# Row sums of softmax weights: a TensorE product with ones against folding by accumulating transfers

## Chip, cores and metric

The kernel runs on one core of a Trainium2 chip, in single precision. The metric is the device time of one execution in microseconds (us). Before the change it is 2455.27 us, the median of three runs (2454.65 to 2456.39).

## What is computed

Two graph layers with residual and layer norm follow one another. The change touches only the attention of the second: 16 batches, 1024 nodes, 256 channels in 4 heads.

```python
# x: 16 x 1024 x 256 after the first layer; adj: 1024 x 1024
g  = relu(einsum('bcn,bnm->bcm', transpose(x), adj * A_s(x)) * para)      # queries
k, v = split(x @ kv_w)                                                   # keys, values
attn = softmax(einsum('bhnd,bhmd->bhnm', q, k) * scale, axis=-1)
out  = einsum('bhnm,bhmd->bhnd', attn, v)
x = layernorm(x + out)
```

A softmax row is divided by the sum of its exponentials. The kernel doesn't divide the weights; it divides the output, so it needs, for each head and query, the sum over 1024 keys.

## The kernel before: the parts concerned

The schedule is one long list for 16 batches, software-pipelined: while batch b attends, the rows of batch b + 2 are normalised and the queries, keys and values of batch b + 1 made. A batch is 16 steps; a step does two of eight key blocks of 128 for one pair of heads and half the queries (512, a "half batch"). So four steps are one pair of heads (`NT // 2`), and eight are a half batch. Two steps are a slot, and the loop takes two slots (four steps) per turn: first the pieces put in these slots, then four steps of scores, exponentials, sums and products with the values.

In `scores` keys lie on the partitions and queries in the free dimension, so exponentials of one query are spread over partitions. VectorE adds the key blocks to one tile per pair, 128 partitions x (2 heads x 512 queries):

```python
accp = right("accp", 2)
...
def sums(g):
    b, hf, pair, cp = step(g)
    ...
    if cp == 0:
        ACC[b, hf, pair] = accp.tile([P, 2, FB], F32, tag="acc", name=f"acc{g}")
        nc.vector.tensor_add(ACC[b, hf, pair], E[g, 0], E[g, 1])
    else:
        for a in range(2):
            nc.vector.tensor_add(ACC[b, hf, pair], ACC[b, hf, pair], E[g, a])
```

What is left is a sum over 128 partitions. TensorE makes it with a matrix of ones, four products per half batch, each in its own 32 columns of the array; ScalarE copies the result, and four transfers put eight equal rows per head below the output in DRAM:

```python
def dens(b, hf):
    p = ps_t.tile([P, FB], F32, tag="t", name="pd")
    for pair in range(NP):
        acc = ACC.pop((b, hf, pair))
        for h in range(2):
            k = 32 * (2 * pair + h)
            more = EX.get((b, hf, pair), [])
            for n, t in enumerate(more + [acc]):
                nc.tensor.matmul(p[k : k + 32, :], ones32, t[:, h, :], start=n == 0, stop=n == len(more))
    DT[b, hf] = otp.tile([P, FB], F32, tag="dt", bufs=1, name=f"dt{b}_{hf}")
    nc.scalar.copy(DT[b, hf], p)
    if not by_pe(b, hf):                      # all but the last half batch
        for k in range(HEADS):
            put_o(b, hf, slice(C + k * DR, C + (k + 1) * DR), DT[b, hf][32 * k : 32 * k + DR, :])
```

Output and sums go through DRAM (`put_o`, `fetch_o`) because the way back, with VectorE's 32 x 32 transpose, turns them to one query per partition. `DR` is 8, so the sum of a head arrives as eight equal numbers, of which one is taken:

```python
def finish_a(b, j):
    ...
    nc.vector.transpose(t..., OB.pop((b, j))...)
    nc.vector.reciprocal(rd, t[:, :, C:].rearrange("p a (h r) -> p a h r", r=DR)[:, :, :, 0])
    p = r = t[:, :, :C]
    ...
    nc.vector.tensor_mul(r..., p..., rd...)          # divide
    nc.vector.tensor_add(r, r, x1s.pop((b, j)))      # residual
    mv, rs = ln_stats(sm, r, f"z{b}_{j}")            # moments on VectorE, square root on GpSimd
    ...                                              # two small GpSimd operations
```

GpSimd also scales the rows of batch b + 2 in place, between their load and VectorE's transpose of them:

```python
def bn2_q(b, j):
    y = yts[b, j].rearrange("p a (d n) -> p a d n", n=Q)
    for k, op in enumerate((OP.mult, OP.add)):
        ...
        nc.gpsimd.tensor_tensor(y, y, sc, op)
```

All transfers are issued from the sync engine, in order. The slots of the pieces of one half batch (`t = (hf + 1) * (NC // NH)`, that is 4 and 8 of the 8 slots of a batch):

```python
put(b, t, dens, b, hf)
...
if b * NH + hf < B * NH - 3:
    t_f, t_a, t_b = (t + 1, t + 2 + k, t + 6 + k) if hf == 0 else (t + 1, t + 4 + k, t + 6 + k)
...
put(b, t_f, fetch_o, b, j); put(b, t_a, finish_a, b, j); put(b, t_b, finish_b, b, j)
```

Of the kernel before, what the change touches and what calls it, by code (L numbers as in the profile page):

```python
# [11 lines left out]
OP = mybir.AluOpType  # L12
AX = mybir.AxisListType
# [3 lines left out]
P = 128  # L17
# [5 lines left out]
def gnn_norm_attention_kernel(  # L23
# [16 lines left out]
    nc = tc.nc  # L40
    B, N, C = x.shape
# [5 lines left out]
    NH = N // FB  # L47
# [38 lines left out]
    DR = 8  # L86
# [42 lines left out]
    with ExitStack() as l0:  # L129
# [33 lines left out]
        with ExitStack() as ph1:  # L163
# [9 lines left out]
            for i in range(0, NT, 2):  # L173
                t = hp.tile([P, 2, N], F32, tag="h", name=f"A{i}")
# [29 lines left out]
            for h in range(NH):  # L204
                rows = range(h * KB, (h + 1) * KB)
# [37 lines left out]
            for c in range(HT):  # L243
                p = ps.tile([P, FB], F32, tag="a", name="pw1")
# [3 lines left out]
            for c in range(CT):  # L248
                p = ps.tile([P, FB], F32, tag="a", name="pw2")
# [149 lines left out]
            for f in range(HT):  # L399
                for h in range(NH):  # L400
# [3 lines left out]
                    p = hidden(B - 1, h, f)  # L404
# [5 lines left out]
        right = lambda name, bufs: ctx.enter_context(tc.tile_pool(name=name, bufs=bufs, side="right"))  # L410
        keep = right("keep", 1)
        ldp = right("ldp", LDP)
        accp = right("accp", 2)
        RD = keep.tile([P, B * NT + 1, HEADS], F32, name="RD")
        ones32 = keep.tile([P, 32], F32, name="ones32")
        stq = keep.tile([P, 2, C // Q], F32, name="stq")
# [45 lines left out]
        with ExitStack() as ph2:  # L462
# [69 lines left out]
            for f in range(KF, HT):  # L532
                t = hT[u][:, f, :]
# [5 lines left out]
            for k, pair in enumerate(pairs):  # L539
# [4 lines left out]
                if not ahead:  # L544
                    for j in range(LDP):
                        load(0, j)
                    for j in range(LDP, NT // 2):
                        t = accp.tile([P, 2, FB], F32, tag="acc", name=f"first{j}")
# [14 lines left out]
    NP = HEADS // 2  # L563
# [17 lines left out]
    def fast():  # L581
      with ExitStack() as fx:
# [16 lines left out]
        kTs, qTs, vs, S, E, ACC, O, OT, DT = {}, {}, {}, {}, {}, {}, {}, {}, {}  # L599
# [228 lines left out]
        def by_pe(b, hf):  # L828
            return b == B - 1 and hf == NH - 1

        def attend(g):
            b, hf, pair, cp = step(g)
            if cp == 0:
                O[b, hf, pair] = [ps_t.tile([P, FB], F32, tag="t", name=f"o{g}_{r}") for r in range(2)]
            for a in range(2):
                cb = 2 * cp + a
                for r in range(2):
                    for h in range(2):
                        nc.tensor.matmul(  # L839
                            O[b, hf, pair][r][h * HD : (h + 1) * HD, :],  # L840
                            vs[b][r * HD : (r + 1) * HD, cb, pair * P + h * HD : pair * P + (h + 1) * HD],
                            E[g, a][r * HD : (r + 1) * HD, h, :],
                            start=(cb == 0),
                            stop=(cb == NT - 1),
                        )
                E.pop((g, a))
            if cp == NT // 2 - 1:
                t = otp.tile([P, FB], F32, tag=f"ot{pair}", bufs=1, name=f"ot{g}")
                o = O.pop((b, hf, pair))
                nc.scalar.copy(t, o[0])  # L850
                nc.vector.tensor_add(t, o[1], t)  # L851
                if by_pe(b, hf):
                    OT[b, hf, pair] = t
                else:
                    put_o(b, hf, slice(pair * P, (pair + 1) * P), t)

        def put_o(b, hf, rows_, t):
# [53 lines left out]
        def finish_a(b, j):  # L911
            hf, k = divmod(2 * j, KB)
            pool_r = (rp, "r") if b < B - 1 or not by_pe(b, hf) else (x1p, "x1")
            rd = RD[:, b * NT + 2 * j : b * NT + 2 * j + 2, :]
            if by_pe(b, hf):
                r = pool_r[0].tile([P, 2, C], F32, tag=pool_r[1], name=f"r_{b}_{j}")
                p = OB.pop((b, j))
            else:
                t = pool_r[0].tile([P, 2, CD], F32, tag=pool_r[1], name=f"r_{b}_{j}")
                nc.vector.transpose(  # L920
                    t.rearrange("p a c -> p (a c)"), OB.pop((b, j)).rearrange("p a c -> p (a c)")
                )
                nc.vector.reciprocal(rd, t[:, :, C:].rearrange("p a (h r) -> p a h r", r=DR)[:, :, :, 0])
                p = r = t[:, :, :C]
            if j == NT // 2 - 1 and by_pe(b, hf):

                for a in range(2):
                    for h in range(HEADS):
                        nc.scalar.mul(r[:, a, ts(h, HD)], p[:, a, ts(h, HD)], rd[:, a, h : h + 1])
            else:  # L930
                nc.vector.tensor_mul(
                    r.rearrange("p a (h d) -> p a h d", h=HEADS),
                    p.rearrange("p a (h d) -> p a h d", h=HEADS),
                    rd.unsqueeze(3).to_broadcast([P, 2, HEADS, HD]),
                )
# [47 lines left out]
        NC = NS // 2  # L983
        NK = NT // 2
        at, between = {}, {}

        def put(w, t, f, *a):
            at.setdefault(w * NC + t, []).append((f, a))
# [4 lines left out]
        for b in range(B):  # L993

            for hf in range(NH):
                t = (hf + 1) * (NC // NH)
                put(b, t, dens, b, hf)
                if by_pe(b, hf):
                    put(b, t, recips, b, hf)
                for k in range(KB // 2):  # L1000
                    j = hf * (KB // 2) + k

                    if b * NH + hf < B * NH - 3:
                        t_f, t_a, t_b = (t + 1, t + 2 + k, t + 6 + k) if hf == 0 else (t + 1, t + 4 + k, t + 6 + k)
                    elif not by_pe(b, hf):

                        t_f, t_a, t_b = t, t + 2 * k, t + 2 + 2 * k if b < B - 1 else (t + 2, NC + 1)[k]
                        if b == B - 1 and k == 0:
                            between[(b * NC + t_b) * 2 + NK // 2] = [(finish_b, (b, j))]
                            t_b = None  # L1010
                    else:
                        t_f, t_a, t_b = t, t + 1 + k, t + 2 + k
                    put(b, t_f, back if by_pe(b, hf) else fetch_o, b, j)
                    if t_a == t:
                        between[(b * NC + t) * 2 + NK // 2] = [(finish_a, (b, j))]
                    else:
                        put(b, t_a, finish_a, b, j)
                    if t_b is not None:
                        put(b, t_b, finish_b, b, j)
            if b == 0:  # L1020
                continue

            if b > 1:
                put(b - 2, 2, begin, b)
                for j in range(NT // 2):
                    put(b - 2, j, load, b, j)
                    put(b - 2, j + 1, bn2_q, b, j)
                    put(b - 2, j + 2, rows, b, j)
                    put(b - 2, j + 2, ln1_a, b, j)
                    put(b - 2, j + 3, ln1_b, b, j)  # L1030
                    put(b - 2, j + 3, put_x1, b, j)
                    put(b - 2, 5 + j // 2 * 2, get_x1, b, j)
                    put(b - 2, min(6 + j, NC), x1_v, b, j)
                put(b - 2, NC - 2, means, b)
                put(b - 2, NC - 1, crow, b)

            i = 0
            for t, n in enumerate(WG):
                for i in range(i, i + n):
                    put(b - 1, t, gate, b, i)  # L1040
                i += 1
            kv = [(keys, (b, c, h)) for h in range(NH) for c in range(CT)]
            kv += [(values, (b, j)) for j in range(0, NT, 2)]
            for t, n in enumerate(KV):
                for _ in range(n):
                    f, a = kv.pop(0)
                    put(b - 1, t, f, *a)
            m = 0
            for t, n in enumerate(QG):
                for m in range(m, m + n):  # L1050
                    put(b - 1, NC - len(QG) + t, graph, b, m)
                m += 1
# [3 lines left out]
        nsteps = B * NS  # L1056


        order = (dens, recips, x1_t, finish_a, fetch_o, finish_b, x1_v, rows, ln1_a, ln1_b, put_x1, get_x1, means, load, crow)
        rank = {f: k for k, f in enumerate(order)}  # L1060
        short = (dens, recips, x1_t, back)

# [141 lines left out]
        for t in range(-NC // 2, max(max(at) // 2, nsteps // NK - 1) + 1):  # L1204
# [3 lines left out]
            for k in range(len(now) + 1):  # L1208
                if k == behind and 0 <= g < nsteps:
                    sums(g)  # L1210
                if k < len(now):
                    f, a = now[k]
# [177 lines left out]
```

## Time and profile before

| | before |
|---|---|
| time, median of 3 | 2455.27 us |
| span of the profiled execution | 2454.0 us |
| busy: TensorE / VectorE / ScalarE / GpSimd | 2411.8 / 1811.3 / 1094.8 / 776.9 us |
| mean busy share of the 16 DMA engines (sync queue) | 43.0% |
| TensorE clock granted, mean | 0.995 of full |

The first 880 us are the first layer and the two batch norms; from about 880 us on the attention runs, until 2454 us. In the profile PE is TensorE's matmul, PEld its weight load, DVE VectorE, ACT ScalarE, POOL GpSimd, SPq the sync engine's queue. A group's line gives the line of the kernel, the engine, the operation and "output<-inputs"; a letter L and a number name a line of the kernel. A share of busy time is an average over stages that have different limits.

### The profile page before, as it was taken

Reading aid. Unit: us, or ns where it says so; the run is one execution under the profiler, and the core shown is the slowest. Engines: PE = TensorE matmul, PEld = TensorE weight load, DVE = VectorE, ACT = ScalarE, POOL = GpSimd, SP = SyncE. Lnnn points to the kernel's source line nnn. Section 1 sums busy time; section 2 is a strip of 40 time slices with the busy share of each in tenths; the row PEclk is TensorE's granted clock in tenths of the full one; section 3 lists DMA queues with packets and bytes.
Section 4 is the critical chain, followed back from the end, with each engine's and each line's share of the span. In section 5 each row is a group of like instructions: output and inputs, shape, how many; then the busy total and the mean of one; then the engine's idle time right before and its main releaser. Section 6 shows DMA issues by size and latency. Waiting matters only on the chain. (4 is left out here: it accounts for less than half of the span.)

```text
span 2454.0 us, 33894 instructions
## 1 busy us (share of the span) xinstructions
PE 2411.8 (98%) x12225; PEld 1008.5 (41%) x12225; DVE 1811.3 (74%) x2584; ACT 1094.8 (45%) x1555; POOL 776.9 (32%) x826
## 2 busy tenths in 40 slices
PE   8999999999999899999999999999999999999997
PEld 4444444444344443443434434344343443443432
DVE  5555545556776777888788888888888888888677
ACT  2000000001554455564655646656566565564645
POOL 2222222231556521414224133232332323414013
PEclk9999999999999899999999999999999999999999
DMA  3122122222578543544545545545354453544222
GB/s 137 69 86 103 69 86 103 85 87 86 199 272 278 133 121 83 143 119 112 143 106 129 143 95 146 122 120 144 81 150 114 123 149 89 145 112 118 72 44 56
DMA packets 583951, 292.73 MB, mean 119 GB/s; under 512 B 407528, under 2 KB 556512, under 8 KB 576608
## 3 DMA queue, kind: packets, MB, share of 16 engines
q1 hardware_dynamic: 583776, 290.49, 43.0%
q8 instruction: 98, 1.61, 0.3%
q14 instruction: 77, 0.63, 0.1%
HBM read 194.46 MB, written 95.94 MB: 118 GB/s over the span
## 5 line engine op out<-in xcount | busy, mean ns | idle before, releaser
L809 ACT ACTIVATE e<-s 128x1024 f32<-128x1024 f32 x512 | 496.0, 1020 | 327.5 <-PE s L797 265.4
L824 DVE TENSOR_TENSOR acc<-acc,e 128x1024 f32<-128x1024 f32 x382 | 509.3, 1333 | 112.1 <-ACT e L809 85.4
L797 PE MATMUL s<-qT,kT 64*64 64x512 f32 x4096 | 490.7, 594 | 4.4 <-ACT e L809 1.7
L839 PE MATMUL o<-e,v 64*64 64x512 f32 x4096 | 485.3, 589 | 0.0
L771 PE MATMUL pg<-wg,x 128*128 128x512 f32 x960 | 426.5, 597 | 0.0
L624 POOL TENSOR_TENSOR yt<-yt,stq 128x512 f32<-128x512 f32 x120 | 185.2, 1544 | 406.4 <-DMA yt<-yT 239.8
L771 PEld LDWEIGHTS pg<-wg,x 128*128 128x128 f32 x960 | 178.7, 190 | 238.6 <-issue 237.4
L839 PEld LDWEIGHTS o<-e,v 64*64 64x64 f32 x4096 | 156.6, 133 | 282.9 <-issue 275.2
L797 PEld LDWEIGHTS s<-qT,kT 64*64 64x64 f32 x4096 | 147.1, 133 | 298.5 <-issue 254.2
L107 ACT COPY u<-pa 128x512 f32<-128x512 f32 x15 | 8.8, 586 | 475.3 <-PE pa L313 475.3
L66 POOL TENSOR_SCALAR rs_z<-mv_z 128x2 f32<-128x2 f32 x64 | 18.5, 290 | 470.5 <-DVE mv_z L573 470.4
L730 DVE SCALAR_TENSOR_TENSOR wg<-wg,adj 128x1024 f32<-128x1024 f32 x128 | 163.4, 1308 | 2.8
L313 PE MATMUL pa<-AhT,x 128*128 128x512 f32 x360 | 161.8, 592 | 0.0
L656 ACT ACTIVATE x<-x,nm_a,rs_a 128x256 f32<-128x256 f32 x128 | 75.8, 594 | 171.9 <-POOL nm_a L646 171.4
L851 DVE TENSOR_TENSOR ot<-o,ot 128x512 f32<-128x512 f32 x64 | 44.2, 691 | 127.5 <-ACT ot L850 127.5
L757 PE MATMUL pv<-kvw,x1T 128*128 128x256 f32 x512 | 118.7, 385 | 0.0
L746 PE MATMUL pk<-x1T,kvw 128*128 128x512 f32 x256 | 117.9, 604 | 0.0
L66 POOL TENSOR_SCALAR rs_a<-mv_a 128x2 f32<-128x2 f32 x64 | 38.0, 594 | 236.5 <-DVE mv_a L573 235.2
L344 PE MATMUL ph<-agg,SW 128*128 128x512 f32 x240 | 112.8, 592 | 0.0
L757 PEld LDWEIGHTS pv<-kvw,x1T 128*128 128x128 f32 x512 | 97.1, 192 | 31.8 <-issue 16.2
L313 PE MATMUL pa<-T,sx 128*128 128x512 f32 x240 | 107.9, 592 | 0.0
L313 PEld LDWEIGHTS pa<-AhT,x 128*128 128x128 f32 x360 | 68.4, 190 | 86.1 <-issue 86.1
(198 smaller groups left out, 3147.1 us busy)
## 6 DMA issues: line engine op xcount, KB each, us to landing
adj<-in_adj_dram SPq DMA_DIRECT2D x128, 512.0 KB
h<-hT SPq DMA_DIRECT2D x28, 1024.0 KB
hL<-h SPq DMA_DIRECT2D x28, 1024.0 KB
ob<-o SPq DMA_DIRECT2D x248, 72.0 KB
x<-in_x_dram SPq DMA_DIRECT2D x16, 1024.0 KB
yT<-y SPq DMA_DIRECT2D x64, 256.0 KB
out_dram<-r SPq DMA_DIRECT2D x64, 256.0 KB
xr<-in_x_dram SPq DMA_DIRECT2D x62, 256.0 KB
```

Source lines behind the costliest of these rows:

```text
L313: nc.tensor.matmul(p, xs[n][:, k, :], bs[n][:, k, :], start=(k == 0), stop=(k == KN - 1))
L344: nc.tensor.matmul(p, ws[n][:, ts(f, P)], bs[n], start=True, stop=True)
L624: nc.gpsimd.tensor_tensor(y, y, sc, op)
L656: nc.scalar.activation(r, r, AF.Identity, bias=nm[:, a : a + 1], scale=rs[:, a : a + 1], accum_out=css[b][:, i : i + 1])
L730: nc.vector.scalar_tensor_tensor(t, t, 1.0, adjs[b * NT + i], op0=OP.add, op1=OP.mult)
L746: nc.tensor.matmul(p, kvw[:, k, ts(c, P)], x1Ts[b][:, k, ts(h, FB)], start=(k == 0), stop=(k == CT - 1))
L757: nc.tensor.matmul(p[:, ts(a, C)], x1Ts[b][:, k, ts(j + a, P)], kvw[:, k, C:], start=(k == 0), stop=(k == CT - 1),)
L771: nc.tensor.matmul(pg[b], x1s[b, k // 2][:, k % 2, ts(c, P)], wgs[b, k][:, ts(h, FB)], start=(k == 0), stop=(k == NT - 1))
L797: nc.tensor.matmul(t[r * HD : (r + 1) * HD, h, :], kTs[b, pair][h * HD : (h + 1) * HD, ts(2 * cb + r, HD)], qTs[b, pair, hf][h * HD : (h + ...
L809: nc.scalar.activation(E[g, a], S.pop((g, a)), AF.Exp)
L824: nc.vector.tensor_add(ACC[b, hf, pair], ACC[b, hf, pair], E[g, a])
L839: nc.tensor.matmul(O[b, hf, pair][r][h * HD : (h + 1) * HD, :], vs[b][r * HD : (r + 1) * HD, cb, pair * P + h * HD : pair * P + (h + 1) * HD],
```

## The change

For all half batches but the last three there is no product with ones. Instead the upper half of the tile's partitions is added to the lower half by a transfer that accumulates, issued from GpSimd: 64 partitions on 64, then 32 on 32, 16 on 16 and 8 on 8. Eight partial sums per query and head are left. They are stored where the eight equal rows stood, and `finish_a` adds the eight numbers (one more VectorE reduction) before the reciprocal. A third `accp` buffer is there because a tile stays in use until its sums are stored. The first fold is a piece of the turn after the pair's last sum; the other three stand between that turn's steps; the store follows in the next turn. So the fetch comes two slots later, and for half 0 the first finishing step is moved between steps.

The purpose is to take the products off TensorE.

```diff
-        accp = right("accp", 2)
+        accp = right("accp", 3)
...
+        def by_dma(b, hf):
+            return b * NH + hf < B * NH - 3
+
+        def fold(b, hf, pair, n):
+            acc = ACC[b, hf, pair]
+            nc.gpsimd.dma_start(acc[:n], acc[n : 2 * n], accum_op=OP.add)
+
+        def put_den(b, hf, pair):
+            acc = ACC.pop((b, hf, pair))
+            for h in range(2):
+                r = C + (2 * pair + h) * DR
+                put_o(b, hf, slice(r, r + DR), acc[:DR, h, :])
...
-                nc.vector.reciprocal(rd, t[:, :, C:].rearrange("p a (h r) -> p a h r", r=DR)[:, :, :, 0])
+                den = t[:, :, C:].rearrange("p a (h r) -> p a h r", r=DR)
+                if by_dma(b, hf):
+                    nc.vector.tensor_reduce(rd, den, AX.X, OP.add)
+                    nc.vector.reciprocal(rd, rd)
+                else:
+                    nc.vector.reciprocal(rd, den[:, :, :, 0])
...
-                put(b, t, dens, b, hf)
+                if by_dma(b, hf):
+                    for pair in range(NP):
+
+                        s = b * NC + t + 2 * (pair - NP + 1)
+                        put(0, s + 1, fold, b, hf, pair, P // 2)
+                        for k in range(3):
+                            between.setdefault(2 * s + k, []).append((fold, (b, hf, pair, P // 4 >> k)))
+                        put(0, s + 2, put_den, b, hf, pair)
+                else:
+                    put(b, t, dens, b, hf)
...
                     if b * NH + hf < B * NH - 3:
-                        t_f, t_a, t_b = (t + 1, t + 2 + k, t + 6 + k) if hf == 0 else (t + 1, t + 4 + k, t + 6 + k)
+                        t_f, t_a, t_b = (t + 3, None, t + 6 + k) if hf == 0 else (t + 3, t + 4 + k, t + 6 + k)
+                        if hf == 0:
+                            between.setdefault((b * NC + t + 2) * 2 + 2 * k + 1, []).append((finish_a, (b, j)))
...
-        order = (dens, recips, x1_t, finish_a, fetch_o, ...
+        order = (dens, recips, x1_t, put_den, finish_a, fetch_o, ...
```

More of the change, by code (lines that the diff above doesn't have):

```diff
@@ L1008, in fast @@
                         if b == B - 1 and k == 0:
-                            between[(b * NC + t_b) * 2 + NK // 2] = [(finish_b, (b, j))]
+                            between.setdefault((b * NC + t_b) * 2 + NK // 2, []).append((finish_b, (b, j)))
                             t_b = None
@@ L1014, in fast @@
                     if t_a == t:
-                        between[(b * NC + t) * 2 + NK // 2] = [(finish_a, (b, j))]
-                    else:
+                        between.setdefault((b * NC + t) * 2 + NK // 2, []).append((finish_a, (b, j)))
+                    elif t_a is not None:
                         put(b, t_a, finish_a, b, j)
@@ L1056, in fast @@
         nsteps = B * NS
-        order = (dens, recips, x1_t, finish_a, fetch_o, finish_b, x1_v, rows, ln1_a, ln1_b, put_x1, get_x1, means, load, crow)
+        order = (dens, recips, x1_t, put_den, finish_a, fetch_o, finish_b, x1_v, rows, ln1_a, ln1_b, put_x1, get_x1, means, load, crow)
         rank = {f: k for k, f in enumerate(order)}
```

## The prediction

> **What bounds the kernel now.** I read the page's first part, busy time by engine:
>
> ```profile
> PE 2411.8 (98%) x12225; PEld 1008.5 (41%) x12225; DVE 1811.3 (74%) x2584; ACT 1094.8 (45%) x1555; POOL 776.9 (32%) x826
> ```
>
> TensorE is busy 98% of the span. That is an average over stages, so next I asked for the busy time of each engine in the attention stage alone, 900 to 2300 us, in the order PE, PEld, DVE, ACT, POOL, then granted clock, DMA share and GB/s:
>
> ```profile
> 900.00:2300.00 1400.00, 1398.16 (x8933) 557.40 (x8935) 1163.11 (x1590) 815.41 (x1134) 435.23 (x548) 1.00 0.50 123
> ```
>
> 1398.16 of 1400 us: TensorE never stops there, and the list of waits for TensorE between 900 and 2380 us is empty. VectorE has 237 us (17%) to spare, GpSimd 965 us (69%), the DMA engines half. So in this stage time is the sum of TensorE's work, and whatever is taken from TensorE comes off the end, as long as the others still keep ahead of it.
>
> Third, what the row-sum products cost. Instructions of the tile `pd` (min/median/max ns):
>
> ```profile
> L870 PE MATMUL pd<-acc,ones x256: 592/593/618, 924.0 to 2439.5; 128*32 128x512 f32 x128
> ```
>
> Of these 256 records each lasts 593 ns, but they must not be summed. The timeline of TensorE shows one stage of them (start, duration, group):
>
> ```profile
> 1272.92 1.98 PE L746 MATMUL pk<-x1T,kvw 128*128 128x512 f32 x4
> 1274.84 1.06 PE L870 MATMUL pd<-acc,ones 128*32 128x512 f32 x8
> 1275.84 5.42 PE L746 MATMUL pk<-x1T,kvw 128*128 128x512 f32 x12
> 1281.09 1.89 PE L757 MATMUL pv<-kvw,x1T 128*128 128x256 f32 x8
> ```
>
> One half batch has eight such records (four products, two records each), and they take 1274.84 to 1275.84, 1.00 us, together. There is a little more: the twelve `pk` records after them come at (1281.09 − 1275.84)/12 = 0.44 us each, so the four before should take 1.75 us, but the first `pd` starts 1.92 us after the first `pk`. A `pd` stage so costs 1.00 us plus about 0.17 us of changing over. The next one of the same kind is at 1375.37: a batch lasts 100.5 us, a half batch 50.3 us, one pair of heads (the unit in which sums are made and folded) 25.1 us.
>
> Last, GpSimd, because the new work goes through its queue (groups in that window: busy, mean ns, idle before and its releasers):
>
> ```profile
> L624 POOL TENSOR_TENSOR yt<-yt,stq 128x512 f32<-128x512 f32 x108 | 169.4, 1569 | 383.4 <-DMA yt<-yT 221.6 <-DMA o<-dt 110.0 <-DVE wg L730 47.7
> L66 POOL TENSOR_SCALAR rs_a<-mv_a 128x2 f32<-128x2 f32 x56 | 35.6, 635 | 221.7 <-DVE mv_a L573 220.5
> L66 POOL TENSOR_SCALAR rs_z<-mv_z 128x2 f32<-128x2 f32 x54 | 12.0, 223 | 321.4 <-DVE mv_z L573 321.4
> ```
>
> GpSimd has 435.23/1400 × 25.1 = 7.8 us of work per pair and otherwise waits for a load or for VectorE's moments. Its idle time is plentiful but lies between steps of a chain (scale the rows loaded, normalise) that VectorE waits for.
>
> **What the Trainium skill says.** TensorEngine Tiling (Array Packing), Key Properties: different tiles run in parallel, and changing the tiling mode drains TensorE. The trace agrees: eight 593 ns records in 1.00 us, and 0.17 us lost ahead of them. DMA: Bandwidth & Descriptors, Anatomy of one DMA — SWDGE (gpsimd) path: a DMA issued from GpSimd takes about 2.0 us plus bytes/436 GB/s, most of it waiting for the write to be confirmed. The kernel before issues none from GpSimd, so no run here shows it yet. Same page, Two DMAs through the same engine are not ordered: a DMA that reads what an earlier one wrote needs the issuing engine to wait for the earlier one's semaphore, so the waits between folds fall on GpSimd itself. SBUF — State Buffer, SBUF: two separate sides: GpSimd can't write descriptors while VectorE runs a 2-port operation. Of VectorE's costly groups here only the sign operation (L729, 69 × 846 ns in the window, 4%) and the scaling of queries can be of that kind; the 1.3 us sums have two inputs. I add nothing for it.
>
> **The change part by part.**
> Removed from TensorE: 32 − 3 = 29 half batches × (1.00 + 0.17) us = 34 us, 29 us without the changeover. It lies on the bound.
> Removed from ScalarE: 29 copies of `pd` at 0.589 us, 17 us. ScalarE is 58% busy in the stage: worth nothing directly.
> Added to VectorE: 58 reductions of 8 × 8 numbers. A reciprocal on 8 numbers takes 204 ns and statistics over 256 take 411 ns, so I estimate 0.25 us each, 15 us in all, in 237 us of room: nothing at the end.
> Added to GpSimd's queue: 29 × 2 pairs × 4 folds = 232 transfers, of 256, 128, 64 and 32 KB. By the skill's formula, estimates: 2.6 + 2.3 + 2.15 + 2.1 = 9.1 us per pair; GpSimd itself stands still for the first three, 7 us, and for four issues. That formula is for a copy on free DMA engines; an accumulating transfer reads the destination too, and the engines here are half busy, so I allow up to twice, 18 us. With the 7.8 us of old work that is 17 to 26 us out of 25.1 us. The lower half fits, the upper end doesn't.
> DMA engines: 58 × 480 KB = 28 MB more through engines that move 123 GB/s, about 20 GB/s over the stage. They have the room.
> Moved: the sums go to DRAM once per pair, after the last fold; the fetch of the output for half 0 comes two slots (half a half batch) later, and its first finishing step one and a half steps into the same loop turn. `accp` grows to three, since a sum stays until it is stored.
> Sum: 2455 − 34 = 2421 to 2455 − 29 = 2426 if nothing new is waited for. I choose 2427: the changeover kept in, some 5 us lost to short stalls.
>
> **The rivals.**
> (1) GpSimd becomes late, and VectorE with it. In each pair the first fold stands behind GpSimd's pieces, and the next turn's row scaling stands behind the last fold. In the trace, one turn has GpSimd's last piece end near 1322.9 us and the transpose of the rows that the next scaling feeds start at 1337.5 us: 14.6 us, of which the scaling takes 3.1. A chain up to some 11.5 us is free, a 15 us one delays VectorE by 3 to 4 us, once or twice per batch. VectorE has 17 us idle per batch and TensorE runs some three steps ahead in `e` buffers (six), so this much is absorbed. With an 18 us chain each turn begins with the backlog of the one before, GpSimd is the bound, and 26 − 25 us times 58 pairs plus stalls makes 2480 to 2560 us. For it: the room is nearly used up at the upper end. Against: the chain has to be twice the skill's figure.
> (2) The sync queue is held up. It is in order; the store of the sums waits for the last fold, and loads of rows, adjacency tiles and the output's fetch stand behind it. In the timeline this queue already idles until the attention output is ready (592.7 us in total), so a store that is ready a few us after that costs little. For half 0, though, the fetch and the step that needs it are now in one turn of 25 us: fold, store, read back, about 10 us. I expect VectorE to wait there some us per batch, within its 17 us. If not, 14 batches × 3 us = 42 us would take back the gain: about 2460.
> (3) TensorE's time isn't freed, because the products were hidden in gaps. The empty list of waits and 1398 of 1400 us busy speak against it; then 2455.
>
> **Range and chances.** Without trouble 2421 to 2426; light stalls up to 2440; rival 2 about 2460, rival 1 2480 and up. The gain can't reach 2% (49 us) since only 34 us are taken away, so faster by over 2% gets 0.03. Slower by over 2% (from 2504) needs rival 1 in full: 0.14. Range 2418 to 2488.
>
> **What would show it.** Right: `pd` has 24 + 8 records left; TensorE still above 99% in the stage; batch period 98.2 us instead of 100.5; GpSimd waiting for `acc` transfers without VectorE waiting for `yt`, `x1` or `ob`. Wrong: TensorE waiting for `e` or `qT`, VectorE waiting for DMA `ob` or for GpSimd `yt`, the sync queue waiting long for `acc`, GpSimd with hardly a gap; a fold of more than 5 us from issue to landing would do it.

## The result and the profile after

The changed kernel takes 2622.47 us (median of 4 runs, 2620.83 to 2625.65) against 2455.57 us for the kernel before on the same chip: a ratio of 1.0681, interval 1.0663 to 1.07. It is 167 us slower. The prediction said 2427 us and a range of 2418 to 2488: the measured time lies 134 us above the end of that range.

The products are gone as intended (TensorE has 11993 matmuls instead of 12225). What is left of TensorE's fullness, first on the page (busy time by engine) of the kernel after:

```profile
PE 2439.7 (93%) x11993; PEld 1017.8 (39%) x11993; DVE 1825.0 (70%) x2642; ACT 1081.5 (41%) x1526; POOL 983.3 (38%) x1058
```

and in the stage between 900 and 2300 us, columns as before (PE, PEld, DVE, ACT, POOL, granted clock, DMA share, GB/s):

```profile
900.00:2300.00 1400.00, 1282.12 (x7812) 510.08 (x7811) 1057.72 (x1480) 719.48 (x996) 570.43 (x702) 0.96 0.59 128
```

TensorE was busy for 1398.16 of these 1400 us; now it stands for 118 us of them, does 12.5% fewer matmuls in the same time (224 of the 1121 missing ones are the products themselves), and its granted clock has fallen from 1.00 to 0.96. Its list of waits between 900 and 2380 us was empty; in the kernel after, between 900 and 2500 us, it has two lines (total us, times, longest):

```profile
PE s L797 <- ACT e L809: 72.0, 14, 6.3
PE pk L746 <- DVE x1T L679: 57.8, 14, 4.1
```

One of each per batch. A batch, by the distance of the `pc` products that occur once in each, lasts 112.4 us (median) instead of 100.53. I call the first wait A, the second B.

**Wait A.** The timeline of the turn that handles the second pair of row blocks (start, duration, group, and in brackets the idle time before it and its releaser):

```profile
1812.53 0.94 POOL L839 DMA_DIRECT2D acc<-acc  x1
...
1823.61 0.18 DVE L573 BATCH_NORM_AGGREGATE mv_a<-st_a 128x2 f32<-128x6 f32 x1
...
1823.89 0.81 POOL L839 DMA_DIRECT2D acc<-acc  x1 [2.95 <-DMA acc<-acc]
...
1824.44 2.80 POOL L624 TENSOR_TENSOR yt<-yt,stq 128x512 f32<-128x512 f32 x2
...
1830.47 0.49 POOL L646 TENSOR_SCALAR nm_a<-mv_a,rs_a 128x1 f32<-128x1 f32 x2
...
1830.76 0.60 ACT L656 ACTIVATE x<-x,nm_a,rs_a 128x256 f32<-128x256 f32 x1 [14.12 <-POOL nm_a L646]
...
1831.94 1.91 ACT L809 ACTIVATE e<-s 128x1024 f32<-128x1024 f32 x2
...
1833.00 3.69 PE L797 MATMUL s<-qT,kT 64*64 64x512 f32 x16 [5.78 <-ACT e L809]
```

Read it from the bottom. TensorE waits 5.78 us for exponentials. ScalarE isn't short of time: it stood for 14.12 us at the normalisation of rows (L656), which comes ahead of the exponentials in its order and waits for `nm_a` (the shift that this normalisation adds, made by GpSimd from VectorE's moments `mv_a`). GpSimd makes `nm_a` late because the fold chain, 1812.53 to 1824.44, stands ahead of it in GpSimd's order, and after that the scaling of the next rows and GpSimd's part of a finishing step. The moments are ready at 1823.79, but GpSimd takes them up only at 1829.35, so 5.56 us of the wait are GpSimd's backlog. The rest is older than the change: in the kernel before, the longest wait of this kind is 7.8 us.

**Wait B.** The start of a batch, where the next keys are made:

```profile
1870.52 3.70 PE L746 MATMUL pk<-x1T,kvw 128*128 128x512 f32 x8
...
1871.84 0.77 DVE L936 STREAM_TRANSPOSE r<-ob 128x576 f32<-128x576 f32 x1
...
1875.15 0.40 DVE L572 BATCH_NORM_STATS2 st_z<-r 128x6 f32<-128x256 f32 x1
...
1876.90 1.30 DVE L679 STREAM_TRANSPOSE x1T<-xb 128x512 f32<-128x512 f32 x2
...
1878.34 5.37 PE L746 MATMUL pk<-x1T,kvw 128*128 128x512 f32 x8 [4.12 <-DVE x1T L679]
```

The second finishing step of half 0, which the change put between the last steps of a batch, occupies VectorE from 1871.84 to about 1875.8, and one addition to a row sum follows, so the transposes `x1T` for the keys start at 1876.90, some 5 us after VectorE reached this place.

**The clock.** The windows right before, at and after these waits:

```profile
1815.00:1826.00 11.00, 11.00 (x44) 4.47 (x47) 10.03 (x21) 1.64 (x5) 3.60 (x5) 1.00 0.33 54
...
1833.00:1837.00 4.00, 4.00 (x20) 1.29 (x24) 3.27 (x3) 2.06 (x3) 3.57 (x5) 0.50 0.77 148
1837.00:1841.00 4.00, 4.00 (x36) 1.27 (x32) 1.62 (x2) 1.63 (x2) 0.80 (x1) 0.85 0.70 113
...
1878.00:1884.00 6.00, 5.66 (x11) 2.62 (x12) 5.90 (x7) 1.89 (x3) 3.29 (x4) 0.72 0.84 201
```

After wait A TensorE runs for 4 us at half clock and 4 more at 0.85, after B 6 us at 0.72: 2.0 + 0.6 + 1.7 = 4.3 us lost. The Trainium skill, TensorE: Matmul & The Clock Gate, What's actually happening, says that the clock halves after at least one idle window of about 3.4 us and recovers after at least one busy window of that length. Here the trace agrees: half clock after a wait of 5.78 us, and for about 5 us from the moment work resumed (4 us, and 30% of the next 4). Shorter waits can do the same; the last section has them.

**The sum of a batch.** Per batch, wait A costs 72.0/14 = 5.1 us, B 57.8/14 = 4.1, the clock 4.3; the missing products give back 1.95 (measured below). 5.1 + 4.1 + 4.3 − 1.95 = 11.6, of 11.9 seen. Over the whole: the last `pc` starts at 2416.1 us instead of 2264.1, 152 us later, and from there to the end it is 202.9 instead of 189.9 us, 13 more: 165 us, the difference of the two spans (2619.0 and 2454.0).

**The folds** themselves are near what was estimated. The page's list of transfers (count, size, median us from issue to landing):

```profile
acc<-acc POOLq DMA_DIRECT2D x58, 256.0 KB, 4.4
...
acc<-acc POOLq DMA_DIRECT2D x58, 128.0 KB, 3.2
...
acc<-acc POOLq DMA_DIRECT2D x58, 64.0 KB, 2.9
acc<-acc POOLq DMA_DIRECT2D x58, 32.0 KB, 2.9
```

4.4 + 3.2 + 2.9 + 2.9 = 13.4 us, inside the 9.1 to 18 that was allowed for. The 9.1 that the prediction works out from the skill's formula is too short by a third here, and the measurement decides.

### The profile page after: what moved, and what is told of

It reads as the page before. It is cut to its first block, busy times and chain, and to the rows that moved or that the text cites. A ratio compares the mean times of both kernels' runs of the same rounds, so it can differ in the third digit from the quotient of the medians.

```text
span 2619.0 us, 33966 instructions
## 1 busy us (share of the span) xinstructions
PE 2439.7 (93%) x11993; PEld 1017.8 (39%) x11993; DVE 1825.0 (70%) x2642; ACT 1081.5 (41%) x1526; POOL 983.3 (38%) x1058
## 5 line engine op out<-in xcount | busy, mean ns | idle before, releaser
L824 DVE TENSOR_TENSOR acc<-acc,e 128x1024 f32<-128x1024 f32 x382 | 483.4, 1265 | 157.0 <-ACT e L809 133.7
L797 PE MATMUL s<-qT,kT 64*64 64x512 f32 x4096 | 515.2, 620 | 79.2 <-ACT e L809 76.5
L855 PE MATMUL o<-e,v 64*64 64x512 f32 x4096 | 495.0, 600 | 0.0
L839 POOL DMA_DIRECT2D acc<-acc x232 | 192.4, 845 | 512.1 <-DMA acc<-acc 506.9
L624 POOL TENSOR_TENSOR yt<-yt,stq 128x512 f32<-128x512 f32 x120 | 174.6, 1456 | 128.2 <-DMA yt<-yT 108.0
L746 PE MATMUL pk<-x1T,kvw 128*128 128x512 f32 x256 | 141.1, 704 | 57.8 <-DVE x1T L679 57.8
L656 ACT ACTIVATE x<-x,nm_a,rs_a 128x256 f32<-128x256 f32 x128 | 75.6, 592 | 267.1 <-POOL nm_a L646 267.1
L66 POOL TENSOR_SCALAR rs_z<-mv_z 128x2 f32<-128x2 f32 x64 | 46.9, 733 | 278.7 <-DVE mv_z L573 249.8
L746 PEld LDWEIGHTS pk<-x1T,kvw 128*128 128x128 f32 x256 | 54.4, 222 | 142.9 <-issue 131.3
```

The lines of the kernel that those rows point to most:

```text
L746: nc.tensor.matmul(p, kvw[:, k, ts(c, P)], x1Ts[b][:, k, ts(h, FB)], start=(k == 0), stop=(k == CT - 1))
L797: nc.tensor.matmul(t[r * HD : (r + 1) * HD, h, :], kTs[b, pair][h * HD : (h + 1) * HD, ts(2 * cb + r, HD)], qTs[b, pair, hf][h * HD : (h + ...
L839: nc.gpsimd.dma_start(acc[:n], acc[n : 2 * n], accum_op=OP.add)
L855: nc.tensor.matmul(O[b, hf, pair][r][h * HD : (h + 1) * HD, :], vs[b][r * HD : (r + 1) * HD, cb, pair * P + h * HD : pair * P + (h + 1) * HD],
```

## Experiments

The theory was that A and B are separate faults of order: A from the chain ahead of the row pieces on GpSimd, B from the moved finishing step on VectorE. Rivals: that folds cost what they cost wherever they stand (contention), or that the two waits are one path. In the expectations A and B are the waits above; C is a second path, VectorE to GpSimd to ScalarE, in the turn of the half-0 products, with no slack in the kernel before; D and E are explained where they come up.

### Without the folds, and without the change's other half

`e4_nofold`: the kernel after, with the 232 folds left out (only eight of 128 partitions are summed).

```diff
-            nc.gpsimd.dma_start(acc[:n], acc[n : 2 * n], accum_op=OP.add)
+            pass
```

> Changed kernel without the 232 folds: eight raw partial sums of 128 are stored, the rest is left out, so the output is not the reference's. Theory: A goes as GpSimd is never held, B stays: about 2515 us, like the run that moves the normalisation. Rival (folds cost through DMA engines and the sync queue, and B is their effect too): both stalls go, about 2425 us.

2532.62 us, 1.0315 (1.0294 to 1.0335), 105.4 to 106.2 us per batch. TensorE's waits, 900 to 2300 us:

```profile
PE pk L746 <- DVE x1T L679: 52.3, 13, 4.0
PE s L797 <- ACT e L809: 12.7, 12, 1.1
```

B is there in full, 4.0 us each, without a single fold: it is the order on VectorE. A shrinks from 5.1 to 1.1 us each. So the folds make most of A, and leaving them out is worth 90 us of the 167. ScalarE's longest wait for `nm_a` falls from 14.7 to 9.3 us. The other 77 us belong to the rest of the change; the next run takes its slots alone.

`e5_before_moved`: the kernel before, with products, and only the slots of the change (both fetches two slots later, half 0's first finishing steps between steps).

```diff
-                        t_f, t_a, t_b = (t + 1, t + 2 + k, t + 6 + k) if hf == 0 else (t + 1, t + 4 + k, t + 6 + k)
+                        t_f, t_a, t_b = (t + 3, None, t + 6 + k) if hf == 0 else (t + 3, t + 4 + k, t + 6 + k)
+                        if hf == 0:
+                            between.setdefault((b * NC + t + 2) * 2 + 2 * k + 1, []).append((finish_a, (b, j)))
...
```

> Kernel before, with its products and no folds; only the slots of half 0 are those of the change (fetch two slots later, finishing steps between the steps of the turn before the x1T transposes). Theory (B is an order on VectorE): the stall of 4 us before the keys is there in all 14 batches and some 1.7 us of low clock after it: 2455 + 81, about 2535 us. Rival (B comes only because the folds make the output's fetch late): within 10 us of 2455.

2483.55 us, 1.0113 (1.0093 to 1.0133), 102.31 us per batch. The slots alone cost 28 us, about a third of what was expected: B is only 1.5 us per batch (20.1 us in 13 waits, at most 1.6) and the granted clock stays at 1.00. So the 4 us of B come from the moved step together with something else. I can only argue what: without the products the turn is shorter, and VectorE has one more operation in each finishing step, a reduction of 0.22 us.

### Taking A away, taking B away

`e1_ln1b`: the kernel after; the normalisation of row block 2 (and its store) one slot later, which is the next turn; block 3 already stood in that slot.

```diff
-                    put(b - 2, j + 3, ln1_b, b, j)
-                    put(b - 2, j + 3, put_x1, b, j)
+                    put(b - 2, j + 3 if j < 2 else 6, ln1_b, b, j)
+                    put(b - 2, j + 3 if j < 2 else 6, put_x1, b, j)
```

> Changed kernel; ScalarE's normalisation of the third row block (the one that waits up to 14 us for GpSimd, ahead of the exponentials of its turn) comes one slot later, behind these exponentials. Theory (two stalls per batch, each followed by about 4 us at half clock: A, ScalarE held by GpSimd's folds; B, the x1T transposes standing behind the finishing step that was moved): A goes, B stays; A is 72.0/14 = 5.1 us of stall plus some 2.6 us of low clock per batch, 7.7 x 14 = 108 us: about 2515 us. Rival (sync queue held by the stores of the sums, and fuller DMA engines): nothing but an order on ScalarE is changed, so within 15 us of 2622.

2630.17 us, 1.0712 (1.0691 to 1.0733): A is gone and nothing is gained; TensorE now waits for `x1T`, 114.4 us in 10 waits.

`e12_after_ln`: the same question more gently: only blocks 0 and 2 move, to between the steps of their own turn, behind its first exponentials.

```diff
-                    put(b - 2, j + 3, ln1_b, b, j)
-                    put(b - 2, j + 3, put_x1, b, j)
+                    if j % 2:
+                        put(b - 2, j + 3, ln1_b, b, j)
+                        put(b - 2, j + 3, put_x1, b, j)
+                    else:
+                        g = (b - 2) * NS + 5 + 2 * j
+                        between.setdefault(g, []).extend([(ln1_b, (b, j)), (put_x1, (b, j))])
```

> Changed kernel, only the normalisation of row blocks 0 and 2 on ScalarE moved between the steps of its own turn (not a whole turn later, as in the first run, which made the output's fetch late). Theory: stall A goes, B stays at about 4 us: 2622 - 108, about 2515 us, 2500 to 2540. Rival (with A gone, B grows as in the first run, since the fold chain then ends later within the turn): 2590 to 2630.

2618.13 us, 1.0664 (1.0643 to 1.0686). Again A is gone (0.7 us in all) and B has grown (waits of TensorE and VectorE, 900 to 2300 us):

```profile
PE pk L746 <- DVE x1T L679: 113.4, 11, 13.4
...
DVE r L936 <- DMA ob<-o: 84.9, 11, 10.1
```

What VectorE now waits for is the output read back. The timelines of both kernels say why. The kernel after, from the chain that made A to the finishing step (the first line is the chain of half 0's first pair, the second that of its second pair, then its stored sums and the fetch):

```profile
1812.53 0.94 POOL L839 DMA_DIRECT2D acc<-acc  x1
...
1835.84 0.91 POOL L839 DMA_DIRECT2D acc<-acc  x1
...
1849.98 0.82 SPq L874 DMA_DIRECT2D o<-acc  x2
...
1852.47 4.67 SPq L922 DMA_DIRECT2D ob<-o  x8
```

and the same in this experiment, with the finishing step in the last line:

```profile
1807.99 0.93 POOL L839 DMA_DIRECT2D acc<-acc  x1
...
1835.19 0.94 POOL L839 DMA_DIRECT2D acc<-acc  x1
...
1848.70 0.64 SPq L874 DMA_DIRECT2D o<-acc  x2
...
1851.00 5.75 SPq L922 DMA_DIRECT2D ob<-o  x8
...
1856.29 0.78 DVE L936 STREAM_TRANSPOSE r<-ob 128x576 f32<-128x576 f32 x1 [8.01 <-DMA ob<-o]
```

On GpSimd stand, in order, the first pair's chain, the row pieces of the turn with their waits for VectorE, and the second pair's chain; then store, fetch, finishing step, transposes, keys. From the first chain's start to the keys it takes 1878.34 − 1812.53 = 65.8 us in the kernel after and, with the keys' wait ending at 1872.36, 64.4 us here. (The profile puts this one wait of the keys down to ScalarE, which had itself waited 8.95 us for a load behind that fetch; the other eleven are for `x1T`.) From the second batch on the stretch is 64.9 to 66.2 us in the kernel after and 63.3 to 67.4 us here, with A and without it. So the keys come no earlier when A is taken away. With A, TensorE is held back early, and the read-back has arrived by the time it is wanted (there VectorE has no wait for `ob`); without A it runs ahead and waits at the keys. The theory that A and B are separate faults, with A worth 108 us by itself, fell, and the rival's 2590 to 2630 us came in.

`e2_finish`: B instead: half 0's first finishing steps one and two turns later.

```diff
-                        t_f, t_a, t_b = (t + 3, None, t + 6 + k) if hf == 0 else (t + 3, t + 4 + k, t + 6 + k)
-                        if hf == 0:
-                            between.setdefault((b * NC + t + 2) * 2 + 2 * k + 1, []).append((finish_a, (b, j)))
+                        t_f, t_a, t_b = (t + 3, t + 5 + k, t + 6 + k) if hf == 0 else (t + 3, t + 4 + k, t + 6 + k)
```

> Changed kernel; the two finishing steps of half 0 come in slots t+5 and t+6, behind the x1T transposes, and no longer between steps. Theory: B goes (4.1 us of stall plus some 1.7 us of low clock per batch, 14 x 5.8 = 81 us), A stays: about 2541 us. Rival (sync queue and DMA): within 15 us of 2622.

2518.38 us, 1.0257 (1.0226 to 1.0287), 102.4 to 109.5 us per batch. This cuts the path before the keys, and 104 us come back. TensorE waits for exponentials only (61.9 us in 31 waits), and ScalarE still stands at `nm_a` for up to 13.3 us.

`e3_both`: both edits (e1 and e2).

> Changed kernel with both moves. Theory: neither stall is left and TensorE has 29 products stages less than before: 2422 to 2440 us, faster than the kernel before by 0.6 to 1.4%. Rival (sync queue and DMA): still over 2580.

2544.89 us, 1.0377 (1.036 to 1.0394), 27 us worse than e2 alone. The rows moved to slot 6 bring new waits: ScalarE for `crow` (74.7 us), the values for a copy of keys (21.9 us). Moving pieces turn by turn only moved the queue.

### Why it doesn't come back to 2425: a second path

`e6_finish_ab`: e2, and half 0's last step two slots later.

```diff
-                        t_f, t_a, t_b = (t + 3, t + 5 + k, t + 6 + k) if hf == 0 else (t + 3, t + 4 + k, t + 6 + k)
+                        t_f, t_a, t_b = (t + 3, t + 5 + k, t + 8 + k) if hf == 0 else (t + 3, t + 4 + k, t + 6 + k)
```

> Changed kernel; half 0's finishing steps in slots t+5, t+6 and the last step of each (ScalarE's normalisation) in t+8, t+9, so that ScalarE is not held by GpSimd there. Theory: of the two waits of ScalarE that the run with the moved finishing step showed (96 us for nm of the output, 178 us for nm of the rows) the first goes, and with it about half of the 71 us stall of TensorE and its low clock: 2470 to 2490 us. Rival (DMA, sync queue): no better than 2518.

2520.56 us, 1.0264 (1.0242 to 1.0286): no better than e2.

`e7_fin_nofold`: e6 with the folds left out, as in e4.

> As the run before it, and without the folds (partial sums of 128 partitions are stored unfolded: that part of the sums is left out). Theory: neither A nor B: 2421 to 2432 us, that is the worth of the products alone. Rival (something else of the change costs): 2450 or more.

2468.26 us, 1.0051 (1.0031 to 1.0071), 101.2 us per batch. No products, no folds, no B, and yet slower than before: waits of about 1.1 us for exponentials in two turns of each batch (28.6 us in 26 waits).

`e13_before_noprod`: the schedule before, slot by slot, with nothing but the products left out. Eight of the 128 partial rows are stored unfolded at the old place, so the sums aren't whole.

```diff
...
-                put(b, t, dens, b, hf)
+                if by_dma(b, hf):
+                    for pair in range(NP):
+                        put(b, t, put_den, b, hf, pair)
+                else:
+                    put(b, t, dens, b, hf)
...
```

> Kernel before in its own schedule, but without the 29 stages of products and without folds: eight raw partial sums of 128 are stored at the old place (that part of the sums is left out; accp 3). It measures what taking the products off TensorE is worth by itself. The prediction's step (TensorE's time comes off the end): 2421 to 2426 us. Theory C (in the turn in which half 0's products stood, the wait of ScalarE for GpSimd ahead of the exponentials is as long as TensorE's work, so the time freed there turns into a wait of about 1 us, as in the run without folds and without stalls): only the other half's stage pays, 2455 - 15 = 2440 us, 2436 to 2445.

2439.10 us, 0.9938 (0.9921 to 0.9954), 99.40 us per batch. Removing the products is worth 16.5 us, not 34. About half of the product stages' 2.34 us per batch comes off, 1.13 us. Most of the rest is now idle time of TensorE, 11.6 of 1400 us or 0.8 us per batch. ScalarE's and TensorE's lines, 900 to 2300 us:

```profile
ACT x L656 <- POOL nm_a L646: 171.4, 28, 8.7
...
PE s L797 <- ACT e L809: 6.9, 13, 0.5
```

The first line reads, in the kernel before:

```profile
ACT x L656 <- POOL nm_a L646: 157.9, 28, 7.8
```

So ScalarE already stood 5.6 us each time ahead of exponentials, hidden behind a full TensorE, with about nothing to spare.

`e8_paired`: e6 with other places for folds and half 0's last step one slot earlier: both pairs of a half batch folded together after its last sum, their transfers alternating, so that one lands while the other is issued (four `accp` buffers; one `rp` buffer less for the space).

```diff
+                    s = b * NC + t
                     for pair in range(NP):
-                        s = b * NC + t + 2 * (pair - NP + 1)
-                        put(0, s + 1, fold, b, hf, pair, P // 2)
-                        for k in range(3):
-                            between.setdefault(2 * s + k, []).append((fold, (b, hf, pair, P // 4 >> k)))
+                        put(0, s, fold, b, hf, pair, P // 2)
+                        put(0, s + 2, put_den, b, hf, pair)
+                    for k in range(3):
+                        for pair in range(NP):
+                            between.setdefault(2 * s + k, []).append((fold, (b, hf, pair, P // 4 >> k)))
-                        put(0, s + 2, put_den, b, hf, pair)
...
-                        t_f, t_a, t_b = (t + 3, t + 5 + k, t + 8 + k) if hf == 0 else (t + 3, t + 4 + k, t + 6 + k)
+                        t_f, t_a, t_b = (t + 3, t + 5 + k, t + 7 + k) if hf == 0 else (t + 3, t + 4 + k, t + 6 + k)
```

> All folds are there, but both pairs of a half batch are folded together, after its last sum: GpSimd issues the second pair's fold while the first pair's is under way, and the chains stand behind the third row block's normalisation and not ahead of it (accp 4, rp 3 buffers; finishing steps of half 0 in t+5, t+6). GpSimd waits for two chains in about 15 us in place of two times 12. Theory: neither A nor B: 2422 to 2440 us, faster than the kernel before by 0.6 to 1.4%. Rival (the folds cost through DMA engines or the sync queue, whatever GpSimd's order): 2490 or more.

2490.48 us, 1.0142 (1.0125 to 1.0159), about 102.5 us per batch. It gains 30 us over e6 and misses what was expected; its time is that of the rival (2490 or more). But the row pieces still stand ahead of the exponentials (`nm_a`: 253.0 us in 28 waits), and the next run changes that and nothing about the folds.

### Taking both away

`e10_paired_ln`: e8, with the normalisation of blocks 0 and 2 between steps (the diff of e12).

> The run with both pairs folded together, and besides the normalisation of row blocks 0 and 2 on ScalarE comes between the steps of its turn, after three of its eight exponentials are issued for, and not ahead of all. Theory C: the stalls of 1.5 and 1.1 us per batch in the two turns go, 14 x 2.6 = 36 us and some for the changeover: 2440 to 2455 us. Rival (the folds cost TensorE or the DMA engines directly): stays near 2490.

2448.41 us (2439.93 to 2460.74), 0.9973 (0.9961 to 0.9985), 98.58 us per batch and in some batches 102.5 to 103.4. `e11_ln_nofold` is e10 with the folds left out:

> As the run before it, without the folds (raw partial sums of 128 are stored, the rest of each sum is left out). Theory C: no stall is left, 98.3 us per batch, 2422 to 2432 us. Rival: 2445 or more.

2431.44 us, 0.9904 (0.9884 to 0.9924), 98.58 us in every batch. Here is what the products were worth with no wait in their place: 100.53 − 98.58 = 1.95 us per batch, 24 us in the whole time. And the same edit as in e12, which changed nothing there, took 42 us off here: the wait at `nm_a` costs only where no longer path lies behind it.

What the longer batches of e10 wait for (waits, 900 to 2300 us):

```profile
ACT wg L720 <- DMA crow<-crow_d: 27.9, 12, 6.3
```

`crow` is the row of means, a load in the sync queue, behind half 0's fetch, which is behind the store of folded sums. Either the queue's order holds it up, or the DMA engines are too full of folds. `e15_fetch_late` puts the fetch of half 0 behind `crow` and its finishing steps to match:

```diff
-                        t_f, t_a, t_b = (t + 3, t + 5 + k, t + 7 + k) if hf == 0 else (t + 3, t + 4 + k, t + 6 + k)
+                        t_f, t_a, t_b = (t + 4, (None, t + 6)[k], t + 7 + k) if hf == 0 else (t + 3, t + 4 + k, t + 6 + k)
+                        if t_a is None:
+                            between.setdefault((b * NC + t + 4) * 2 + 1, []).append((finish_a, (b, j)))
```

> The fastest whole version so far, in which some batches take 102.5 us and not 98.6 because ScalarE waits up to 6 us for the row of means, whose transfer stands behind the output's fetch in the sync queue. Here half 0's fetch comes one slot later, behind the row of means, and its first finishing step between the steps of the next turn. Theory: all batches at about 98.6 us, 2430 to 2442 us, with less spread between runs. Rival (the row is late because the DMA engines are full of folds): stays at 2445 to 2455.

2440.15 us (2439.22 to 2441.04), 0.9935 (0.9919 to 0.9952), with all folds in it and all sums whole: 182 us faster than the kernel after and 0.65% faster than the one before. Every batch takes 98.58 us, the wait for `crow` is gone, and the stage is full again at a DMA share of 0.64:

```profile
900.00:2300.00 1400.00, 1395.31 (x8882) 566.78 (x8884) 1165.83 (x1658) 812.99 (x1123) 618.45 (x772) 1.00 0.64 143
```

So it was the order of the queue. In steady batches the folds now cost nothing. The last `pc` is at 2236.6 us, 27.5 earlier than before; but from there to the end it takes 200.8 us instead of 189.9. In the last batch, timeline of e15:

```profile
2372.06 2.07 ACT L969 ACTIVATE r<-r,nm,rs_z 128x256 f32<-128x256 f32 x4 [7.27 <-POOL nm L961]
...
2375.09 3.69 PE L797 MATMUL s<-qT,kT 64*64 64x512 f32 x16 [7.49 <-ACT e L809]
```

It is wait A's pattern once more: finishing steps of two half batches meet in one turn, ScalarE stands at a GpSimd result ahead of exponentials, and TensorE loses 7.49 us and then runs at half clock (3.69 us for 16 records, 1.9 otherwise). Most of the 10.9 us are there. Spreading these steps wasn't tried.

### One more fold

These two have a fifth fold, 4 partitions on 4, on each chain; the eight rows stored then no longer add up to the sum. With `e14_fifth_fold` on the kernel after I wanted to know how much of the chains lies on the path: both chains of half 0 in full (D), or one fold per batch (E).

```diff
-                        for k in range(3):
+                        for k in range(4):
```

> Changed kernel with a fifth fold (4 partitions on 4) behind the four of each pair, 58 transfers of 16 KB more; the sums stored are no longer whole. A fold costs GpSimd about 3.7 us (0.8 to issue, 2.9 to land). Theory D (A and B are two places at which one serial path through a batch shows: chain of pair 0, row normalisation, chain of pair 1, store, fetch, finishing step, x1T, keys; that is why taking A away left 112 us per batch): both chains lie in it, 7.4 us per batch more, 2622 + 104, about 2725 us, 2700 to 2750. Rival E (two stalls independent of each other, only A is made by the folds): A grows by 3.7 us, 2622 + 52, about 2674 us or less.

2673.70 us, 1.0886 (1.0864 to 1.0907): 51 us more, 3.7 us per batch, about the size of one fold, issue included. Wait A grows from 5.1 to 7.7 us. D fell, and E's 2674 us was met; but not E's reason, for if the two waits were independent of each other, e12 would have gained A's 108 us. In the trace, from the first chain's start (1841.42) to the end of the keys' wait (1910.59) there are 69.2 us instead of 65.8. The second chain has slack: in the kernel after the read-back was complete before VectorE came to it, and here VectorE begins to wait for it (18.7 us in 10 waits, 0.76 us in that batch).

`e16_paired_fifth`: the same on e10.

> The fastest whole version so far (both pairs folded together, normalisation between steps) with the same fifth fold. Theory D: its chains are off the path, the 58 transfers more cost nothing: 2440 to 2462 us, as without them. Rival (folds cost by themselves, through GpSimd's issue or the DMA engines): 2500 or more.

2511.92 us, 1.0227 (1.0206 to 1.0247), far above what was expected and where the rival had it (2500 or more): e10 had no slack for one fold more. Waits of ScalarE and of the sync queue, 900 to 2300 us:

```profile
SPq L874 <- DMA acc<-acc: 126.3, 53, 7.7
...
ACT wg L720 <- DMA crow<-crow_d: 83.8, 12, 9.6
```

The store of the sums is held up longer (it was 55.9 us in e10), and `crow` behind it three times as long: the same queue that e15 puts in order. A fifth fold on e15 wasn't run, so how much room its order leaves isn't known.

## Why the prediction was wrong

**The bound** was read rightly, and one conclusion from it was wrong: "whatever is taken from TensorE comes off the end, as long as the others still keep ahead of it". An engine that is 99.9% busy hides any other path that is just as long. e13 shows one: of 34 us of products 16.5 come off.

**Removed from TensorE, 29 × (1.00 + 0.17) = 34 us**: in size nearly right. Where nothing takes its place it is 1.95 us per batch, 28 us for 14.5 batches; the 0.20 us per batch by which TensorE is less full in e11 and e15 than before (1395.31 instead of 1398.16 of 1400 us) would make it 2.15, against 2.34 predicted. 29 us, without the changeover, was the better figure.

**ScalarE's copies, VectorE's reductions**: right for e15, which has them and runs as fast per batch as e11. A reduction takes 0.22 us (0.25 estimated). Whether those two in front of the keys add to B is open.

**The fold chain** of 9.1 to 18 us: right, 13.4 by landing times and 11.9 us until GpSimd goes on.

**The step that failed** is in the first rival: "A chain up to some 11.5 us is free, a 15 us one delays VectorE by 3 to 4 us, once or twice per batch", and "this much is absorbed". It asked which VectorE work waits for GpSimd, the row scaling, and never which ScalarE work does. Behind the chain in GpSimd's order stands `nm_a`, ScalarE waits for it ahead of its exponentials, and TensorE for those. The room ahead of `nm_a` can be read in the very turn of the kernel before from which the 11.5 us were taken (GpSimd's two waits there):

```profile
1330.24 0.22 POOL L66 TENSOR_SCALAR rs_z<-mv_z 128x2 f32<-128x2 f32 x1 [5.21 <-DVE mv_z L573]
...
1332.91 1.02 POOL L66 TENSOR_SCALAR rs_a<-mv_a 128x2 f32<-128x2 f32 x1 [1.00 <-DVE mv_a L573]
```

The free room was 5.21 + 1.00 = 6.2 us (6.2 to 8.1 over the batches), not 11.5, and a chain of 11.9 us overruns it by 5.7. That is about what GpSimd is late in wait A (5.56 us) and what TensorE waits there (5.78 us). So next to nothing was absorbed: ScalarE already stood ahead of its exponentials for up to 7.8 us, with about nothing to spare (e13), and now stands 14.12. The sign was in the profile before: 157.9 us of ScalarE waiting for `nm_a`, 28 times. "Against: the chain has to be twice the skill's figure" fell with it: 1.5 times (13.4 against 9.1 us) was enough.

**The second rival** had the right suspect, the read-back of half 0 in one turn, and the wrong victim. In the kernel after VectorE doesn't wait for `ob`. The finishing step, listed under "Moved" and priced at nothing, stands ahead of the keys' transposes: 4.1 us per batch (B). Only when A is away does VectorE wait for the read-back, 8 to 9 us on average and at most 10.4 (e1, e12).

**Not in the prediction at all**: two chains and the row pieces between them on one in-order queue, then store, fetch and finishing step, make a path of about 65 us from the first chain's start to the keys, which has slack behind the second chain while A stands (e14) and sets the pace once A is gone (e1, e12); and a clock that halves after each of the waits, 4.3 us per batch.

**What would show it**: "TensorE waiting for `e`" was on the list of signs of a wrong prediction, and it is the first line of the waits after; GpSimd with hardly a gap, on the same list, isn't seen (38% busy). Its waits, not its load, did the damage. With "1398 of 1400" read as safety the range ended at 2488, and slower by over 2% got 0.14.

**What stays open**: why B alone is 1.5 us in e5 and 4.0 in e4, which differ in the products (what I name there is argued, not tested), and the part of the 13 us in the last batches of the kernel after that isn't wait A and half clock, which I didn't follow.

## What to carry over

Before you move work to an idle engine, list everything that stands behind the new waits in that engine's order, and follow each result to its consumer and to what stands behind the consumer: 11.9 us on GpSimd, idle two thirds of the time, had 6.2 us of room and became 5.8 us on TensorE by way of ScalarE. A full engine hides paths of its own length, so leave the work out without putting anything in its place before estimating a gain (e13: 16.5 instead of 34 us). When removing a wait changes nothing (e12), look for the same path ending elsewhere rather than for a new cause: compare the times between the same events in both timelines.

## What the runs showed of the hardware

The transfers that accumulate cost little less when they get smaller: 64 KB and 32 KB both take 2.9 us from issue to landing (median), and 16 KB, in e14, 2.7 us. Each of the 232 in the kernel after holds GpSimd 0.77 to 1.15 us for its issue, 0.845 us on average. 256 KB takes 4.4 us (median) and up to 8.4; the slowest was issued at 1996.5 us, and from 1996 to 2005 us the DMA share was 0.97.

After a wait TensorE's granted clock can fall to 0.50 for spells of about 3.4 us or multiples of it. Between 900 and 2300 us each wait of 4.0 us or more, in all runs, brought such a spell, and no wait of up to 1.8 us did (e5, e7 and e13 have no longer ones and no spell). In between it went both ways: in e2, a wait of 1.93 us ahead of 1349.01 us is followed by a clock of 0.50 from 1349.5 to 1352.9 us, while 25 of the 26 waits of e8, up to 2.7 us, have no such spell. So a wait shorter than the idle window quoted above can be enough; where the two differ, the measurement decides. The stage's mean clock is 1.00 in e5 and e7 and 0.99 in e3, where the longest wait is 2.6 us; it is 0.98 in e4 (4.0 us), 0.96 in the kernel after (6.3) and 0.95 in e12 (13.4).
